# Graph attention in two layers: one fill order for the score banks, one exponential over two banks, and four smaller moves

## The chip, the cores and the metric

The kernel runs on one core of a Trainium2 chip. The metric is the time on the device in microseconds, as the median of several executions. Before the change it is 15735.61 us (three executions, 15734.61 to 15738.93).

## The reference: what is computed

Two layers on a graph of 3327 nodes with 128 features. The second one takes nearly all the time.

```python
# layer 0: attention by cosine, masked by the adjacency, residual, layernorm
cos = beta[0] * (x @ x.T) / (norm2 @ norm2.T + 1e-07)
x = _layernorm(x + softmax(cos + (1.0 - adj) * -1e9) @ x)
# layer 1: q, k, v have the shape (d, n, h) = (128, 3327, 8): 128 heads of 8 features
q = (x @ Wq.T).reshape(d, n, h)
k = (x @ Wk.T).reshape(d, n, h)
v = (x @ Wv.T).reshape(d, n, h)
a = einsum('dnh,dmh->dnm', q, k) * scale + adj + adj
out = einsum('dnm,dmh->dnh', softmax(a, axis=2), v)
x = _layernorm(x + out.reshape(n, h * d) @ Wo.T)
```

## The kernel before, in words

The nodes are padded to 26 tiles of 128. The work has four stages.

**Layer 0** (up to some 704 us) goes tile by tile through a pipeline written out by hand. Besides its own work it turns the adjacency (`adj_chunk`) and stores it in bf16 as `aT_s`, one DMA for each query tile, of 128 rows of 6,656 bytes (L215), and it stores q, k and v.

**Preparation** (704 to some 987 us): `prepare`, called 16 times, loads 16 heads of k or q (L796), lets GpSimd reorder them (L798), turns them on TensorE, splits each value into a high and a low part (L810, L811) and stores both (L818). Between its calls the adjacency of the first query block is loaded (L507) and exponentiated (L514), and the first maxima are searched for.

**The attention loop** (987 to some 15613 us) is the main stage. A unit is a block of query tiles with a group of four heads: 9 blocks by 32 groups make 288 units. Eight blocks have three tiles (384 query columns), the last has two (256). A unit has 26 steps, j = 0 to 25, one for each tile of 128 keys, so that there are 288 x 26 = 7488 steps. The maximum over the keys is needed before the scores can be exponentiated, so the scores are computed twice: once in a search for the maxima, which runs T + AHEAD = 33 steps ahead, and once to be used. The search for two units takes 52 steps, and each step searches one *pair* (two heads with 512 keys each, PSUM tile m2, two banks, L613) and one *single* (one head with 512 keys, PSUM tile m1, one bank, L634); `max_steps` lists which. In a two-tile block every second step has no pair. The maxima, negated and split into three bf16 parts by `shift_parts`, become the "shift" of a unit, which `shift_turn` turns on TensorE (L663) in the steps j = 22 to 24 of the unit before, into columns 384 to 511 of a bank of ea, out of which ScalarE copies it (L914, tile cx).

TensorE, ScalarE, VectorE and GpSimd execute exactly in the order in which the code issues (a manual schedule); only the DMA queue of SP is ordered by a scheduler. In a step TensorE's order is:

1. shifts of heads 2 and 3 into eb (two banks, L690), the first search, scores of heads 2 and 3 on top (L696). ScalarE exponentiates eb in one instruction (L893), and GpSimd multiplies by the exponentiated adjacency (L894).
2. shifts of heads 0 and 1 into ea (L690), the second search, scores on top (L696), perhaps L663 or L725, then twice the adjacency in eight matmuls, four for each head (L677). ScalarE exponentiates each of the two ea tiles with an instruction of its own (L923), then come the copies out of ea.
3. the weighing of the step before the last with the values (L707).

Heads 0 to 3 lie on four groups of 32 rows of the array, and the heads of a search on those of their own number. The first search is the pair if it is one of heads 0 and 1 (`early`), else the single. Of the 52 steps of a cycle, by the number s of the step modulo 52, the pair comes first in 6 to 31 and the single in the others. In steps 5 and 31 pair and single are on the same two heads. m1 and m2 have one buffer each; ea has two tiles of one bank, which are both in use in each step; eb has one tile of two banks.

When a unit is done, its sums are turned into the free columns of ea in the step j = 20 of the next unit (`values_turn`, L725) and finished in the same step: a copy on ScalarE (L737), a reciprocal on VectorE (L741), a product on GpSimd (L742), a store (L755). The keys of the unit after next are loaded at j = 2 (L530, L535, L542).

**The end** (15613 us on): for each of 26 tiles, eight transposes, copies, sixteen matmul instructions with Wo (L977) and the residual (L978). After the last tile come the rest of the layernorm over all tiles (`layernorm`, L133 to L141) and the store of the result (L983).

## Time and profile before

| | |
|---|---|
| median of three executions | 15735.61 us |
| the profiled execution | 15731.62 us |
| its span | 15729.8 us |
| share of the span busy: PE, DVE, ACT, POOL | 98%, 88%, 81%, 88% |
| layer 0, up to 704 us: DMA share | 0.43 |
| L893, 128x768 (6656 times): mean | 811 ns |
| L923, 128x384 (13312 times): mean | 490 ns |
| L613, 128x1024: mean | 1219 ns |
| L634, 128x512: mean | 684 ns |
| L894, 128x768: mean | 1843 ns |

PE is TensorE's matmuls, PEld its weight loads, DVE VectorE, ACT ScalarE, POOL GpSimd, SP the queue that issues the DMAs. A line such as "L893 ACT ACTIVATE pb<-eb" names the line of the code, the engine, the operation, what it writes and what it reads. Rows of the timeline begin with the start in us from the span's start and the duration in us; neighbouring instructions of one kind are merged ("x2"), and a bracket tells of the engine's idle time before it. Matmuls are pipelined, so that several of them overlap and the ends that the trace shows for them are modelled.

### The profile page before, as it was taken

Reading aid. Unit: us, or ns where it says so; the run is one execution under the profiler, and the core shown is the slowest. Engines: PE = TensorE matmul, PEld = TensorE weight load, DVE = VectorE, ACT = ScalarE, POOL = GpSimd, SP = SyncE. Lnnn points to the kernel's source line nnn. Section 1 sums busy time; section 2 is a strip of 40 time slices with the busy share of each in tenths; the row PEclk is TensorE's granted clock in tenths of the full one; section 3 lists DMA queues with packets and bytes.
Section 4 is the critical chain, followed back from the end, with each engine's and each line's share of the span. In section 5 each row is a group of like instructions: output and inputs, shape, how many; then the busy total and the mean of one; then the engine's idle time right before and its main releaser. Section 6 shows DMA issues by size and latency. Waiting matters only on the chain.

```text
span 15729.8 us, 508048 instructions
## 1 busy us (share of the span) xinstructions
PE 15442.3 (98%) x217532; PEld 6909.7 (44%) x217532; DVE 13882.2 (88%) x16261; ACT 12687.4 (81%) x24930; POOL 13894.1 (88%) x9571
## 2 busy tenths in 40 slices
PE   8879999999999999999999999999999999999999
PEld 6644444444444444444444444444444444444555
DVE  7679999999999999999999999999999999998775
ACT  7658888888888888888888888888888888888776
POOL 0059999999999999999999999999999999999886
PEclk9989999999999999999999999999999999999999
DMA  4451111111111111111111111111111111111112
GB/s 169 180 201 49 45 49 52 49 46 49 52 50 49 47 50 52 49 45 49 52 49 46 49 53 48 50 45 56 45 49 45 49 52 49 46 49 60 61 56 74
DMA packets 600521, 951.50 MB, mean 60 GB/s; under 512 B 283090, under 2 KB 515408, under 8 KB 557808
## 3 DMA queue, kind: packets, MB, share of 16 engines
q1 hardware_dynamic: 598256, 918.99, 18.0%
q8 instruction: 1703, 27.90, 0.7%
q14 instruction: 562, 4.60, 0.1%
HBM read 784.19 MB, written 134.61 MB: 58 GB/s over the span
## 4 chain that ended last, share of the span: by engine, by line
PE 91%; DVE 2%; ACT 1%; issue 0%; POOL 0%; DMA 0%; SPq 0%; ACTq 0%; DVEq 0%; POOLq 0%
PE acc L707 29%; PE ea L677 20%; PE m L598 15%; PE eb L690 12%; PE ea L690 9%; PE ea L696 2%; PE eb L696 2%; PE ea L663 1%; DVE mx L613 1%; PE ea L725 1%; DVE mx L634 1%; ACT pa L923 0%; PE pp L977 0%; POOL pb L894 0%; ACT pb L893 0%
## 5 line engine op out<-in xcount | busy, mean ns | idle before, releaser
L894 POOL TENSOR_TENSOR pb<-pb,eT 128x768 f32<-128x768 f32 (+1 forms) x7488 | 13206.6, 1781 | 752.7 <-ACT pb L893 557.7
L613 DVE TENSOR_REDUCE mx<-m 128x2 f32<-128x1024 f32 x6784 | 8271.6, 1219 | 506.9 <-PE eb L696 283.1
L893 ACT ACTIVATE pb<-eb 128x768 f32<-128x768 f32 (+1 forms) x7488 | 5895.6, 787 | 2509.9 <-PE eb L696 1716.6
L598 PE MATMUL m<-kx,qx 32*128 32x512 f32 (+1 forms) x23296 | 6774.5, 471 | 85.9 <-DVE mx L613 78.2
L923 ACT ACTIVATE pa<-ea 128x384 f32<-128x384 f32 (+1 forms) x14976 | 6339.0, 478 | 56.5 <-PE ea L677 43.5
L707 PE MATMUL acc<-pb,vt 128*9 128x384 f32 (+1 forms) x29952 | 5904.2, 474 | 0.1
L707 PE MATMUL acc<-pa,vt 128*9 128x384 f32 (+1 forms) x29952 | 5903.3, 474 | 0.0
L634 DVE TENSOR_REDUCE mx<-m 128x1 f32<-128x512 f32 x6400 | 4377.6, 684 | 682.2 <-PE m L598 316.3
L690 PEld LDWEIGHTS <-one 3*128 3x128 bf16 x29952 | 1508.1, 91 | 5553.9 <-issue 4650.8
L677 PE MATMUL ea<-aT,two 128*32 128x384 bf16 (+1 forms) x59904 | 3716.2, 325 | 0.0
L696 PE MATMUL eb<-qx,kx 32*128 32x384 f32 (+1 forms) x14976 | 3444.5, 452 | 0.0
L696 PE MATMUL ea<-qx,kx 32*128 32x384 f32 (+1 forms) x14976 | 3439.1, 437 | 0.0
L690 PE MATMUL ea<-cx,one 3*128 3x384 bf16 (+1 forms) x14976 | 3293.0, 322 | 2.3
L598 PEld LDWEIGHTS m<-kx,qx 32*128 32x128 f32 x23296 | 2813.9, 182 | 443.7 <-DVE mx L613 123.0
L690 PE MATMUL eb<-cx,one 3*128 3x384 bf16 (+1 forms) x14976 | 2462.7, 326 | 1.3 <-ACT pb L893 0.6
L707 PEld LDWEIGHTS acc<-pa,vt 128*9 128x9 f32 x29952 | 1416.7, 91 | 781.5 <-issue 0.3
L677 PEld LDWEIGHTS <-two 128*32 128x32 bf16 x59904 | 947.0, 95 | 1415.6 <-issue 1273.6
L696 PEld LDWEIGHTS eb<-qx,kx 32*128 32x128 f32 x14976 | 1461.7, 189 | 0.0
L696 PEld LDWEIGHTS ea<-qx,kx 32*128 32x128 f32 x14976 | 1433.1, 182 | 8.0 <-issue 3.0
L707 PEld LDWEIGHTS acc<-pb,vt 128*9 128x9 f32 x29952 | 1418.8, 91 | 0.6 <-POOL pb L894 0.6
L638 DVE TENSOR_REDUCE mx<-m 128x2 f32<-128x512 f32 x1088 | 747.9, 687 | 96.3 <-PE eb L696 38.2
L116 POOL MEMSET raw<- 128x1 f32 x26 | 2.4, 98 | 559.0 <-DVE mn L260 478.2
(126 smaller groups left out, 5253.8 us busy)
## 6 DMA issues: line engine op xcount, KB each, us to landing
kx<-kp_s SPq DMA_DIRECT2D x576, 832.0 KB
vn<-v_s SPq DMA_DIRECT2D x288, 416.0 KB
qx<-qp_s SPq DMA_DIRECT2D x1024, 48.0 KB
raw<-in_adj_dram SPq DMA_DIRECT2D x25, 1663.5 KB
aT_s<-aT SPq DMA_DIRECT2D x26, 832.0 KB
aT<-aT_s SPq DMA_DIRECT2D x208, 96.0 KB
q_s<-row SPq DMA_DIRECT2D x26, 512.0 KB
k_s<-row SPq DMA_DIRECT2D x26, 512.0 KB
```

Of the source, the lines that this page charges most:

```text
L598: nc.tensor.matmul(dst, u.qx[rows(a), q * P : (q + 1) * P], u.kx[rows(a), k0:k1], start=True, stop=True,)
L613: nc.vector.tensor_reduce(u.mx[:, h, qs[0], c], m, axis=AX.X, op=ALU.max)
L634: nc.vector.tensor_reduce(u.mx[:, a, qs[0], c : c + 1], m, axis=AX.X, op=ALU.max)
L638: nc.vector.tensor_reduce(u.mx[:, a, qs[0] : qs[1] + 1, c], m.rearrange("p (q k) -> p q k", q=2), axis=AX.X, op=ALU.max,)
L663: nc.tensor.matmul(dst[r], parts[u.i % 2][:, q, h], unit, start=start, stop=True, tile_position=(0, 32 * h), skip_group_check=True,)
L677: nc.tensor.matmul(e[r, : u.nq], two[:, r], aT[:, j, : u.nq], start=False, stop=True, tile_position=(0, 32 * c), skip_group_check=True,)
L690: nc.tensor.matmul(e[:, : u.nq], one[r], u.cx[r, : u.nq], start=True, stop=False, skip_group_check=True)
L696: nc.tensor.matmul(e[:, : u.nq], u.kx[rows(a), j * P : (j + 1) * P], u.qx[rows(a), : u.nq], start=False, stop=stop, skip_group_check=True,)
L707: nc.tensor.matmul(acc[32 * h : 32 * h + H + 1, : u.nq], u.vt[:, h, j], pts[h // 2][:, h % 2, : u.nq], start=(j == 0), stop=(j == T - 1), ...
L893: nc.scalar.activation(pt_b[:, :, : u.nq], e_b[:, :, : u.nq], AF.Exp)
L894: nc.gpsimd.tensor_tensor(pt_b[:, :, : u.nq], pt_b[:, :, : u.nq], eT[:, j, : u.nq].unsqueeze(1).to_broadcast([P, 2, u.nq]), ALU.mult,)
L923: nc.scalar.activation(pt_a[:, h, : u.nq], e[:, : u.nq], AF.Exp)
```

## The change

It has five parts.

1. **Fill order.** In three-tile blocks the pair is always the first search, and the single the second. The pair's heads are now those of ea (`hs_a`), and the other two those of eb (`hs_b`), so that ea and eb change heads when the pairs do. The list of singles is reordered so that no single has a head of the pair beside it. In the two-tile block the order stays as it was: single first, pair second, eb with heads 2 and 3.
2. **One exponential.** ea becomes one tile of two banks with one buffer, and one ACTIVATE exponentiates both.
3. **The sums of a finished unit** are turned at j = 8 in place of 20, with their copy (`leave`), and the reciprocal and what follows (`finish`) come one step later, at j = 9.
4. **Loads.** `aT_s` is laid out by query block, so that a store of one query tile is made of pieces of 256 bytes, and a load of one key tile of pieces of 768 bytes in place of 256. In the preparation the heads are loaded two calls ahead, and the loads of the adjacency are spread over four calls, seven tiles in each.
5. **The end.** The layernorm is done tile by tile inside the loop, and the first 20 tiles are stored while the last six are computed.

```diff
-    aT_s = dram.tile([T, P, T, P], BF16, name="aT_s")
+    aT_s = dram.tile([NB, P, T, QT * P], BF16, name="aT_s")
...
     def layernorm(dst: bass.AP, src: bass.AP):
-        stats = small.tile([P, T, nc.vector.BN_STATS_DIM], F32, name="ln_stats", bufs=1)
...
+        stats = small.tile([P, nc.vector.BN_STATS_DIM], F32, name="ln_stats")
+        mv = small.tile([P, nc.vector.BN_AGGR_DIM], F32, name="ln_mv")
+        rstd = small.tile([P, 1], F32, name="ln_rstd")
+        nc.vector.bn_stats(stats, src)
+        nc.vector.bn_aggr(mv, stats)
+        nc.vector.tensor_scalar(rstd, mv[:, 1:2], EPS, None, op0=ALU.add)
         nc.scalar.activation(rstd, rstd, AF.Sqrt)
         nc.vector.reciprocal(rstd, rstd)
...
             if c == NCH - 1:
-                nc.sync.dma_start(aT_s[t], u.aT)
+                q = t % QT
+                nc.sync.dma_start(aT_s[t // QT][:, :, q * P : (q + 1) * P], u.aT)
...
-            nc.sync.dma_start(
-                aT[:, j, :w].rearrange("p (q n) -> p q n", n=P),
-                aT_s[b * QT : b * QT + w // P, :, j].rearrange("q p n -> p q n"),
-            )
+            nc.sync.dma_start(aT[:, j, :w], aT_s[b][:, j, :w])
...
             pairs = [(u, lo, *k) for k in full[:12]] + [(u, lo, (2,), 6)]
-            ones = one(u, hi, full[13:] + [left]) + one(u, lo, full[12:] + [left])
+            last = one(w, hi, full[12:] + [left])
+            ones = one(u, hi, full[13:] + [left]) + last[:1] + one(u, lo, full[12:] + [left])
             pairs += [(u, hi, *k) for k in full[:13]] + [(u, hi, (2,), 6)]
             pairs += [(w, hi, *k) for k in full[:12]]
-            ones += one(w, lo, full[13:] + [left])
             pairs += [(w, lo, *k) for k in full[:13]]
-            ones += one(w, hi, full[12:] + [left])
+            ones += one(w, lo, full[13:] + [left]) + last[1:]
...
+        def search(step):
+            if step is not None:
+                (max_pair if len(step[1]) == 2 else max_single)(*step)
...
-                    pts[h // 2][:, h % 2, : u.nq],
+                    pts[h][:, : u.nq],
...
+        def leave(u, src):
+            u.of = sm.tile([P, QT, 4, H + 1], F32, name="of")
+            nc.scalar.copy(u.of[:, : u.nt].rearrange("p q h r -> p (q h r)"), src[:, : 36 * u.nt])
+
+        def finish(u):
+            by = u.of.rearrange("p q h r -> p h q r")[:, :, : u.nt]
...
+                load_heads(0)
+                load_heads(1)
+                for i in range(len(works)):
+                    prepare(i)
...
+                    if i % 2 and i < 9:
+                        for j in range(7 * (i // 2), min(7 * (i // 2) + 7, T)):
                             load_adj_tile(0, j)
...
-            ps_a = at.enter_context(tc.tile_pool(name="at_a", bufs=2, space=PSUM))
+            ps_a = at.enter_context(tc.tile_pool(name="at_a", bufs=1, space=PSUM))
...
             def new_a():
-                return [ps_a.tile([P, 512], F32, name="ea") for _ in range(2)]
+                return ps_a.tile([P, 2, 512], F32, name="ea")
...
-                    early = pair is not None and pair[1] == (0, 1)
+
+                    full = pair is not None and width(units[pair[0]][0]) == QB
+                    first = pair if full else single
+                    late = single if full else pair
+                    hs_a = pair[1] if full else (0, 1)
+                    hs_b = tuple(h for h in range(4) if h not in hs_a)
...
-                    shifts(u, b01, (2, 3))
-                    if early:
-                        max_pair(*pair)
-                    elif single is not None:
-                        max_single(*single)
-                    scores(u, j, b01, (2, 3), True)
+                    shifts(u, b01, hs_b)
+                    search(first)
+                    scores(u, j, b01, hs_b, True)
...
-                    e_a = new_a()
-                    shifts(u, e_a, (0, 1))
-                    if early:
-                        max_single(*single)
-                    elif pair is not None:
-                        max_pair(*pair)
-                    scores(u, j, e_a, (0, 1), False)
+                    both = new_a()
+                    e_a = [both[:, x] for x in range(2)]
+                    shifts(u, e_a, hs_a)
+                    search(late)
+                    scores(u, j, e_a, hs_a, False)
...
-                    if j == T - 6 and done is not None:
+                    if j == 8 and done is not None:
                         values_turn(done, free, False)
-                        copies.append(lambda: finish(done, free))
+                        copies.append(lambda: leave(done, free))
+                    if j == 9 and done is not None:
+                        copies.append(lambda: finish(done))
...
-                    for h, e in enumerate(e_a):
-                        nc.scalar.activation(pt_a[:, h, : u.nq], e[:, : u.nq], AF.Exp)
+                    nc.scalar.activation(pt_a[:, :, : u.nq], both[:, :, : u.nq], AF.Exp)
...
-            nc.vector.tensor_add(hid[:, t, :], pp, x1)
-        res = big.tile([P, T, D], F32, name="res")
-        layernorm(res, hid)
-        rf = res.rearrange("p t d -> p (t d)")
+            hid = work.tile([P, D], F32, name="hid1")
+            nc.vector.tensor_add(hid, pp, x1)
+            layernorm(res[:, t, :], hid)
+            if t == HALF - 1:
+                nc.sync.dma_start(node_blocks(out, slice(0, P), HALF * D), rf[:, : HALF * D])
```

## The prediction

> **What bounds the kernel now.** I read the totals of the page, then busy time by stage, then the timeline of single steps in two places.
>
> ```profile
> span 15729.8 us, 508048 instructions
> PE 15442.3 (98%) x217532; PEld 6909.7 (44%) x217532; DVE 13882.2 (88%) x16261; ACT 12687.4 (81%) x24930; POOL 13894.1 (88%) x9571
> ```
>
> PE is near its span, but its matmuls overlap, so 98% doesn't say that PE is the limit. By stage (columns: length, busy PE, PEld, DVE, ACT, POOL, clock, DMA share, GB/s):
>
> ```profile
> 704.00:987.00 283.00, 127.79 (x554) 92.46 (x554) 135.93 (x215) 76.50 (x145) 51.37 (x30) 0.62 0.95 332
> 987.00:14260.00 13273.00, 13250.56 (x189309) 5562.42 (x189309) 12121.84 (x13742) 10969.24 (x21304) 12629.08 (x8394) 1.00 0.16 49
> 14260.00:15613.00 1353.00, 1352.35 (x23517) 686.47 (x23509) 1027.61 (x1327) 1090.90 (x2770) 1195.59 (x1101) 1.00 0.18 56
> ```
>
> The time lies in the second row: 256 units of three query tiles, 6656 steps of 2.00 us on average. The third row is the last 32 units, of two tiles. The first is the preparation, bound by DMA (share 0.95). What limits a step is seen in a steady pair of them:
>
> ```profile
> 8001.88 0.34 PE L690 MATMUL eb<-cx,one 3*128 3x384 bf16 x2
> 8001.89 0.50 PE L598 MATMUL m<-kx,qx 32*128 32x512 f32 x2
> 8002.43 1.23 DVE L613 TENSOR_REDUCE mx<-m 128x2 f32<-128x1024 f32 x1
> 8003.58 0.68 DVE L634 TENSOR_REDUCE mx<-m 128x1 f32<-128x512 f32 x1
> 8004.31 0.49 PE L598 MATMUL m<-kx,qx 32*128 32x512 f32 x1
> 8005.82 0.34 PE L690 MATMUL eb<-cx,one 3*128 3x384 bf16 x2
> ```
>
> It is a ring: pair matmuls to pair reduction 0.54, to single reduction 1.15, to the single matmul that waits for bank m1 0.73, to the start of the next-but-one step 1.51. That is 3.94 us for two steps, 1.97 each. Neither DVE nor PE is full; the ring through both sets the pace.
>
> In the steps j = 22 to 24 ScalarE also copies the next unit's shifts (L914) out of the bank that the score tile ea lies in, and another ring is in force:
>
> ```profile
> 7290.25 0.50 PE L598 MATMUL m<-kx,qx 32*128 32x512 f32 x1
> 7290.74 0.50 PE L677 MATMUL ea<-aT,two 128*32 128x384 bf16 x8
> 7291.19 0.87 ACT L923 ACTIVATE pa<-ea 128x384 f32<-128x384 f32 x2
> 7291.95 0.27 ACT L914 CAST cx<-ea 128x128 bf16<-128x128 f32 x1
> 7292.17 0.42 PE L690 MATMUL ea<-cx,one 3*128 3x384 bf16 x2
> 7292.27 0.50 PE L598 MATMUL m<-kx,qx 32*128 32x512 f32 x1
> ```
>
> From single to single 0.94 + 0.76 + 0.32 = 2.02 us: the first exponential starts 0.45 us after the adjacency matmuls begin, and the second shift of the next step waits until the copy has left the bank.
>
> **What the skill says.** "ScalarE: Activation LUTs", section on what ACT_TABLE_LOAD costs: an ACTIVATE without pointer operands takes 186 ns and 0.833 ns per element, and neighbours overlap by some 93 ns. The trace agrees: 0.811 us for 768 elements (826 by the page), 0.49 for 384, overlap 0.11. So one exponential over two banks saves only 2 x 0.49 - 0.11 - 0.81 = 0.06 us of ScalarE. "TensorE: Matmul & The Clock Gate", Part 3 (the mechanism): matmuls on different row groups run together. The trace agrees: L598 starts 7 ns behind L690. "DMA: Bandwidth & Descriptors", Specifications: below 512 B a transfer falls short of line rate. The trace has 18 ns for packets of 256 B against 254 ns for 6,656 B, 1.8 times the time per byte.
>
> **The change, part by part** (against the profiled execution, 15731.6 us; its span lacks 1.8 us of that, and the median of the three runs, 15735.6, lies 4.0 above it).
>
> *Constant fill order and singles off the pair's heads.* The ring has the same length in either order: steps s mod 52 = 6 to 17 (pair first) average 1.970 us from one L893 start to the next, 32 to 45 (single first) 1.965. Only the crossings cost. Over the 128 cycles of 52 steps (two units, counted from the first one's step 0), steps 4 and 5 take 4.45 where two take 3.94, steps 30 to 33 take 8.37 where four take 7.87: 1.01 us. Step 30 has four short matmuls that remain, 0.1; and the half with pair first is 0.27 us longer than the other without its crossing, and will now come twice. I take 0.80 gone per cycle (bounds 0.65 and 0.92): 128 x 0.80 = **-102**.
>
> *One exponential over two banks.* It waits for both heads' adjacency matmuls. These start in two groups of four, 0.17 us apart (row by row in the trace), so where PE ends the wait it starts 0.17 later, and both banks come free together. Queued behind it on ScalarE are the copies and the next L893; for the banks PE waits with the next ea shifts, and behind those stand the single, the scores, the adjacency and the weighing, that is, the whole step. In the copy ring: 0.94 + 0.17 = 1.11 to the exponential, 0.81 - 0.11 = 0.70 to the copy, 0.32 + 0.02 to the next single: 2.15 against 2.02. Three such intervals a unit: 256 x 3 x 0.13 = **+100**. In plain steps this ring is 0.63 (ea shift to the last add) + 0.44 + 0.81 + 0.05 (end of the exponential to the shift it frees) = 1.93, under the 1.97 of the other: nothing, but with 0.04 us to spare. That cover is thin: each 0.01 beyond it costs up to 6656 x 0.01 = 67.
>
> In the two-tile units the ring already shows: in a step without a pair the second ea shift starts 0.05 us after the second exponential ends.
>
> ```profile
> 14751.04 0.66 ACT L923 ACTIVATE pa<-ea 128x256 f32<-128x256 f32 x2
> 14751.40 0.28 PE L690 MATMUL eb<-cx,one 3*128 3x256 bf16 x2
> 14751.47 0.55 PE L690 MATMUL ea<-cx,one 3*128 3x256 bf16 x2
> ```
>
> One exponential of 512 elements starts 0.12 later (14751.16), takes 0.60 as L893's does there, and frees both at 14751.81 where the second shift started at 14751.75. With 0.01 in the other step: 0.07 per two steps, 416 x 0.07 = +30; the copies of two steps in 32 units, 64 x 0.13 = +8: **+38**.
>
> *Values turned at j = 8, finished at 9.* L725 costs the same PE time, 0.22, at either place. Its copy holds the bank, so step 9 gets the 0.13 of the copy ring, which step 21 had in part: +0.15 us. The reciprocal L741 no longer waits for ScalarE (58 us in 162 waits in the three-tile units); behind it on DVE the pair reduction was late by 0.07. Net +0.09 for each of 256 units: **+23** (bounds -20 and +45).
>
> *Layout of aT_s, loads two ahead.* Each store of a tile in the first layer becomes 3328 pieces of 256 B instead of 128 of 6,656: 3328 x 18 / 16 = 3.7 us of all engines against 2.0. Today it lands 3.4 us after its issue and the next write into its buffer comes some 16.8 us after that issue: hidden, with 13 us to go; it also sits ahead of nothing urgent, as the raw tiles land 20 us early. On SP nothing is reordered in the main loop but o_s<-ob, now ahead of vn, which waits longer anyway. In the preparation the first adjacency loads fall from 9984 packets of 18 ns to 3328 (768 B, an estimate of 37 from 39 at 832 B): -3.5; the earlier loads fill gaps of a stage that is 0.95 full, at most 15. A load two ahead waits on SP for GpSimd to have emptied its buffer, with the stores of the piece in hand behind it; those need the output of the same copy, so they lose nothing. I take **-5** (bounds -15 and +5).
>
> *Layernorm tile by tile.* The chain ends in 26 L141 in a row, 6.5 us, then 1.66 MB out in 6.9. Afterwards one L141 and six tiles' bytes are left: -6.2 and about -4 (0.39 MB at 330 GB/s instead of 1.66), +1.3 where the table load, hidden today, comes in front of a copy. DVE has room: 1.3 us of new work in a period of 3.355. **-9**.
>
> Sum: -102 + 100 + 38 + 23 - 5 - 9 = +45: **15780**.
>
> **Rivals.** *The crossings win* (chance 0.18). If the joint exponential starts no later than the pair of them (ScalarE busy until then, as in steady steps where L893's end holds it back), the +100, the +30 and the +8 vanish and the reciprocal's gain stays: 15735.6 - 102 - 20 - 14 = 15600. For it: in the shorter step of a plain pair the first exponential starts at the end of L893 (8005.30 after 8004.60 + 0.81, less the overlap). Against it: in the copy steps and the two-tile units it starts 0.45 and 0.40 after the adds begin.
> *The ea ring becomes the bound everywhere* (0.12). It decides from 1.97 per step, that is if the joint exponential starts over 0.04 later than I put it: at 0.06 more it is 1.99, and some 40 of 52 steps lose 0.02: 128 x 40 x 0.02 = +102, so 15882. Speaking for it: shift, score, add, exponential are one buffer deep.
> *The crossings stay* (0.08): where the heads change sides the first step could stall just as now; 15780 + 102 = 15882.
>
> **How the numbers follow.** The forecast holds with 0.62, between 15690 and 15850: sums of the bounds above (-16 and +20 for the crossings, +-40 for the copies, +-45 for the finish, partly cancelling). About 0.2% (31 us) is what a measurement of this kernel can tell from no change. Slower by more than that: 0.38 of the forecast's 0.62, and the two slow rivals: 0.58. Within: 0.20. Faster: the rival's 0.18 and 0.04 of the forecast: 0.22. Signs are mixed, so the range reaches out: 15620 to 15880.
>
> **What would show it.** Right: steps 4, 5 and 31 at the length of the others; copy steps of 2.15 us, the two-tile pair of steps 3.10 instead of 3.03; joint exponentials of 0.81 whose start stands 0.44 after the last add; the last L141 some 1.5 us after the last matmul. Wrong: copy steps still at 2.02 (then the first rival), plain steps above 1.97 with PE's ea shifts waiting for the exponential (the second), DVE waits as many as now (the third), or time gained or lost ahead of 987 us by more than 15.

## The result and the profile after

The changed kernel takes **15764.5 us** (median of 20 runs, 15757.6 to 15773.0) against 15734.6 for the kernel before (20 runs, 15731.3 to 15739.9): ratio **1.0019**, 95% interval 1.0012 to 1.0026. It is 30 us slower where 45 were forecast (15780). The profiled execution took 15766.6 us.

The totals of the page are nearly those of before; only the number of instructions fell, by one exponential a step.

```profile
span 15764.8 us, 500738 instructions
PE 15460.4 (98%) x217532; PEld 7036.6 (45%) x217532; DVE 13904.7 (88%) x16311; ACT 12722.1 (81%) x17467; POOL 13895.4 (88%) x9571
```

So the reading has to be by stage again. I cut the stages at the first exponential of eb (L905, L893 before), at the first of the two-tile units and at the last. Columns: length, busy PE, PEld, DVE, ACT, POOL, clock, DMA share, GB/s.

```profile
704.00:996.27 292.27, 141.86 (x569) 97.48 (x569) 137.48 (x216) 77.64 (x148) 51.38 (x30) 0.58 0.94 322
996.27:14351.13 13354.86, 13303.24 (x190378) 5721.43 (x190374) 12183.94 (x13808) 11076.19 (x14792) 12702.69 (x8447) 1.00 0.16 49
14351.13:15659.25 1308.12, 1303.45 (x22436) 651.27 (x22432) 976.50 (x1261) 1013.82 (x1794) 1123.33 (x1048) 1.00 0.18 54
```

Before, the same cuts give 988.4 to the first exponential, 13346.6, 1278.0 and a tail of 116.9. So the 35 us between the two profiled spans are +7.8 ahead of the loop, +8.3 in the three-tile units, +30.2 in the two-tile units, and -11.3 in the tail (105.6).

The small +8.3 is a sum of large terms. The crossings, the steps at which pair and single used to change places, no longer cost time: the starts of L905 in steps 4, 5 and 6 of one cycle stand 1.92 and 2.02 us apart. In the same cycle of the kernel before they stood 2.17 and 2.28 apart, with ScalarE idle for up to 0.70 ahead of them. Before, then after:

```profile
7254.15 0.81 ACT L893 ACTIVATE pb<-eb 128x768 f32<-128x768 f32 x1 [0.40 <-PE m L598]
7256.32 0.81 ACT L893 ACTIVATE pb<-eb 128x768 f32<-128x768 f32 x1 [0.59 <-PE m L598]
7258.60 0.81 ACT L893 ACTIVATE pb<-eb 128x768 f32<-128x768 f32 x1 [0.70 <-PE m L598]
```

```profile
7265.52 0.81 ACT L905 ACTIVATE pb<-eb 128x768 f32<-128x768 f32 x1 [0.30 <-PE eb L692]
7267.44 0.81 ACT L905 ACTIVATE pb<-eb 128x768 f32<-128x768 f32 x1 [0.29 <-PE eb L692]
7269.46 0.81 ACT L905 ACTIVATE pb<-eb 128x768 f32<-128x768 f32 x1 [0.30 <-PE eb L692]
```

A copy step (one in which ScalarE copies a shift of the next unit out of ea), in the timeline of the same kernel:

```profile
7301.13 0.50 PE L590 MATMUL m<-kx,qx 32*128 32x512 f32 x1
7301.62 0.50 PE L673 MATMUL ea<-aT,two 128*32 128x384 bf16 x8
7302.23 0.81 ACT L934 ACTIVATE pa<-ea 128x768 f32<-128x768 f32 x1
7302.94 0.26 ACT L924 CAST cx<-ea 128x128 bf16<-128x128 f32 x1
7303.25 0.34 PE L686 MATMUL ea<-cx,one 3*128 3x384 bf16 x2
7303.26 0.50 PE L590 MATMUL m<-kx,qx 32*128 32x512 f32 x1
```

From single to single 2.13 us: 0.49 to the adds, 0.61 to the joint exponential, 0.71 to the copy, 0.32 to the next single. The joint exponential starts when the second group of adds is through, the copy stands behind it, and TensorE's next shift into ea stands behind the copy. Before, the same interval was 2.02.

Two-tile steps, same view:

```profile
14669.78 0.60 ACT L905 ACTIVATE pb<-eb 128x512 f32<-128x512 f32 x1 [0.29 <-PE m L590]
14669.88 0.40 PE L673 MATMUL ea<-aT,two 128*32 128x256 bf16 x8
14670.40 0.60 ACT L934 ACTIVATE pa<-ea 128x512 f32<-128x512 f32 x1
14671.05 0.28 PE L686 MATMUL ea<-cx,one 3*128 3x256 bf16 x1
...
14671.39 0.60 ACT L905 ACTIVATE pb<-eb 128x512 f32<-128x512 f32 x1 [0.40 <-PE m L590]
...
14672.88 0.60 ACT L905 ACTIVATE pb<-eb 128x512 f32<-128x512 f32 x1 [0.29 <-PE m L590]
```

The pair of steps takes 3.10 us, and the next shift into ea comes 0.05 after the joint exponential's end (14671.00).

### The profile page after: what moved, and what is told of

It reads as the page before. It is cut to its first block, busy times and chain, and to the rows that moved or that the text cites. A ratio compares the mean times of both kernels' runs of the same rounds, so it can differ in the third digit from the quotient of the medians.

```text
span 15764.8 us, 500738 instructions
## 1 busy us (share of the span) xinstructions
PE 15460.4 (98%) x217532; PEld 7036.6 (45%) x217532; DVE 13904.7 (88%) x16311; ACT 12722.1 (81%) x17467; POOL 13895.4 (88%) x9571
## 4 chain that ended last, share of the span: by engine, by line
PE 92%; ACT 1%; issue 0%; DVE 0%; DMA 0%; POOL 0%; ACTq 0%; SPq 0%; POOLq 0%; DVEq 0%
PE acc L703 29%; PE ea L673 20%; PE m L590 15%; PE eb L686 12%; PE ea L686 12%; PE ea L692 2%; PE ea L659 1%; PE eb L692 1%; ACT pa L934 1%; PE ea L721 1%; ACT pb L905 0%; PE pp L994 0%; DVE oT L147 0%; DMA qp_s<-low 0%; PE tp L157 0%
## 5 line engine op out<-in xcount | busy, mean ns | idle before, releaser
L905 ACT ACTIVATE pb<-eb 128x768 f32<-128x768 f32 (+1 forms) x7488 | 5894.0, 787 | 1975.5 <-PE eb L692 1218.8
L590 PE MATMUL m<-kx,qx 32*128 32x512 f32 (+1 forms) x23296 | 6944.4, 473 | 80.4 <-DVE mx L605 72.1
L934 ACT ACTIVATE pa<-ea 128x768 f32<-128x768 f32 (+1 forms) x7488 | 5896.6, 787 | 599.6 <-PE ea L673 283.1
L686 PEld LDWEIGHTS <-one 3*128 3x128 bf16 x29952 | 1825.0, 91 | 5841.7 <-issue 4753.9
L686 PE MATMUL ea<-cx,one 3*128 3x384 bf16 (+1 forms) x14976 | 2487.7, 319 | 55.4 <-ACT pa L934 9.2
## 6 DMA issues: line engine op xcount, KB each, us to landing
raw<-in_adj_dram SPq DMA_DIRECT2D x25, 1663.5 KB, 6.5
```

The lines of the kernel that those rows point to most:

```text
L590: nc.tensor.matmul(dst, u.qx[rows(a), q * P : (q + 1) * P], u.kx[rows(a), k0:k1], start=True, stop=True,)
L686: nc.tensor.matmul(e[:, : u.nq], one[r], u.cx[r, : u.nq], start=True, stop=False, skip_group_check=True)
L905: nc.scalar.activation(pt_b[:, :, : u.nq], e_b[:, :, : u.nq], AF.Exp)
L934: nc.scalar.activation(pt_a[:, :, : u.nq], both[:, :, : u.nq], AF.Exp)
```

## The experiments

All times are medians; ratios are to the kernel before, run on the same chip (15730.4 to 15732.0 there, up to 4 us under the 15734.6 that the changed kernel was compared with). Two tables carry the verdicts. The first is read like the windows above, from the starts of the exponential of eb; its last column is the median of all executions, the others are of the profiled one. The second is read from the mean distances of these starts at each of the 52 places of a cycle (two units), summed over the places named. A cycle occurs 128 times.

```
kernel                  first exp  three-tile  two-tile  tail    total
before                    988.4     13346.6     1278.0   116.9   15734.6
after                     996.3     13354.9     1308.1   105.6   15764.5
e8_order_alone            983.5     13236.6     1277.5   117.3   15615.6
e2_joint_alone            983.7     13453.5     1306.5   116.5   15866.7
e5_values_moved           987.5     13334.3     1279.3   117.1   15721.3
e6_outside_loop           998.6     13344.3     1278.3   106.0   15720.7
e1_two_exps               992.4     13231.2     1280.2   105.9   15617.3
e7_two_exps_old_prep      991.5     13235.9     1279.9   105.8   15618.1
e4_old_order              987.8     13456.4     1308.1   105.8   15865.5
e3_copy_elsewhere         996.6     13248.1     1298.4   105.4   15647.9
e9_joint_held             991.1     13336.7     1300.9   105.4   15735.1
e10_two_exps_held         997.6     13251.6     1294.3   105.2   15648.3
e11_joint_in_plain        988.4     13416.0     1358.4   106.5   15876.6
e12_two_exps_one_wait     987.9     13218.3     1271.5   105.1   15587.0
```

```
us per cycle        steps 4,5,30-33  22-25,48-51  8,9,34,35  20,21,46,47  other 30
                    (crossings)      (copies)     (values)
before                  12.82          16.19        7.87        8.33        59.06
after                   11.85          16.78        8.50        8.08        59.13
e8_order_alone          11.82          16.17        7.88        8.43        59.11
e2_joint_alone          12.79          16.81        7.87        8.56        59.08
e5_values_moved         12.82          16.14        8.09        8.05        59.07
e1_two_exps             11.82          16.14        8.30        8.03        59.07
e4_old_order            12.79          16.77        8.41        8.06        59.10
e3_copy_elsewhere       11.85          15.93        8.53        8.07        59.11
e9_joint_held           11.83          16.77        8.49        8.03        59.08
e10_two_exps_held       11.82          16.25        8.30        8.05        59.10
e11_joint_in_plain      11.85          17.12        8.63        8.11        59.10
e12_two_exps_one_wait   11.85          16.00        8.18        8.11        59.12
```

The last column is the first thing to see: 30 plain steps take 59.1 us, 1.97 each, in every kernel. No edit here moved them by more than 0.07 us in 59. That the ring through the search is their limit, as the prediction has it, is read from the timelines: no edit here changes that ring.

### The exponential split again in the changed kernel (e1_two_exps)

```
-            ps_a = ...(name="at_a", bufs=1, space=PSUM)
+            ps_a = ...(name="at_a", bufs=2, space=PSUM)
...
-                return ps_a.tile([P, 2, 512], F32, name="ea")
+                return [ps_a.tile([P, 512], F32, name="ea") for _ in range(2)]
...
-                    nc.scalar.activation(pt_a[:, :, : u.nq], both[:, :, : u.nq], AF.Exp)
+                    for h, e in enumerate(e_a):
+                        nc.scalar.activation(pt_a[:, h, : u.nq], e[:, : u.nq], AF.Exp)
```

> The changed kernel with one edit undone: two exponentials of one bank each, as before, in place of the joint one; the fill order, the choice of heads, the moved values, the preparation and the tail stay as changed. My theory (the order gains, the joint exponential gives it back): by the terms on record 15764.5 - 100 - 38 = 15627 us; sized by the two traces instead (copy steps' excess 1.02 us per cycle of 52 steps against 0.43, two-tile units +30): 15764.5 - 128 x 0.59 - 30 = 15659. Copy steps 2.02 to 2.06, two-tile pair of steps 3.03. Rival (the joint exponential costs nothing, and the order gains less than its crossings show): 15765, all steps as in the changed kernel.

Measured: 15617.3 us (15611.7 to 15623.0), ratio 0.9928 (0.9915 to 0.9940). A copy step, from its timeline:

```profile
7239.31 0.50 PE L673 MATMUL ea<-aT,two 128*32 128x384 bf16 x8
7239.76 0.87 ACT L934 ACTIVATE pa<-ea 128x384 f32<-128x384 f32 x2
7240.52 0.27 ACT L923 CAST cx<-ea 128x128 bf16<-128x128 f32 x1
7240.73 0.42 PE L686 MATMUL ea<-cx,one 3*128 3x384 bf16 x2
```

From the adds to the first exponential 0.45 where the joint one needs 0.61, to the copy 0.76 where it needs 0.71. So the joint exponential, with the tile of two banks that it reads, costs 147 us of the changed kernel (144 if each is set against the kernel before on its own chip). The two profiled executions lie 155 apart: 124 in the three-tile units, 28 in the two-tile units, and 4 ahead of the loop, where this edit does nothing. The order's gain was there all along.

### The joint exponential alone (e2_joint_alone)

The same edit, the other way round, in the kernel before (with one buffer in place of two):

```
-                return [ps_a.tile([P, 512], F32, name="ea") for _ in range(2)]
+                return ps_a.tile([P, 2, 512], F32, name="ea")
...
-                    for h, e in enumerate(e_a):
-                        nc.scalar.activation(pt_a[:, h, : u.nq], e[:, : u.nq], AF.Exp)
+                    nc.scalar.activation(pt_a[:, :, : u.nq], both[:, :, : u.nq], AF.Exp)
```

> The kernel before with one edit alone: the score tile ea as one tile of two banks and one exponential over it. My theory: 15734.6 + 100 + 38 = 15873 us by the terms on record, 15734.6 + 76 + 30 = 15841 as sized by the traces; the crossings stay at 4.45 and 8.37 us or grow a little. Rival (the joint exponential costs nothing): 15735. A second rival (in the half with the single first, where the second search of a step is the pair, the joint exponential's later end stalls plain steps too): above 15900.

Measured: 15866.7 us, ratio 1.0087 (1.0073 to 1.0100), +136. The copy steps grow by 0.62 per cycle, the two-tile units by 28.5 us, the plain steps not at all: the second rival is out.

### The old order in the changed kernel (e4_old_order)

```
-            last = one(w, hi, full[12:] + [left])
-            ones = one(u, hi, full[13:] + [left]) + last[:1] + one(u, lo, full[12:] + [left])
+            ones = one(u, hi, full[13:] + [left]) + one(u, lo, full[12:] + [left])
...
-                    hs_a = pair[1] if full else (0, 1)
-                    hs_b = tuple(h for h in range(4) if h not in hs_a)
+                    early = pair is not None and pair[1] == (0, 1)
+                    first, late = (pair, single) if early else (single, pair)
+                    hs_a, hs_b = (0, 1), (2, 3)
```

> The changed kernel with one edit undone: the fill order of before (pair first in half of the steps, single first in the other, heads 0 and 1 always in ea); the joint exponential and all else stay. My theory: the crossings come back, + 102: 15867 us; steps 4, 5 at 4.45 together and 30 to 33 at 8.37. Rival (crossings were paid for elsewhere, in the half with the pair first, and the order is worth nothing): 15765.

Measured: 15865.5 us, ratio 1.0086 (1.0072 to 1.0099). The crossing is back, here at steps 4 and 5, 2.14 and 2.28 us. The brackets show ScalarE idle for up to 0.77 ahead of the exponential of eb, where it was 0.30 in the changed kernel, and the search's matmul (L589) as what it came behind:

```profile
7305.07 0.81 ACT L902 ACTIVATE pb<-eb 128x768 f32<-128x768 f32 x1 [0.30 <-PE eb L691]
7307.21 0.81 ACT L902 ACTIVATE pb<-eb 128x768 f32<-128x768 f32 x1 [0.51 <-PE m L589]
7309.49 0.81 ACT L902 ACTIVATE pb<-eb 128x768 f32<-128x768 f32 x1 [0.77 <-PE m L589]
```

The order is worth 101.6 us (13456.44 - 13354.86) in the three-tile units, with joint exponential and moved values.

### The order alone (e8_order_alone)

The edit of e4 the other way round in the kernel before; two exponentials and values at j = 20 stay:

```
-            ones = one(u, hi, full[13:] + [left]) + one(u, lo, full[12:] + [left])
+            last = one(w, hi, full[12:] + [left])
+            ones = one(u, hi, full[13:] + [left]) + last[:1] + one(u, lo, full[12:] + [left])
...
+                    hs_a = pair[1] if full else (0, 1)
+                    hs_b = tuple(h for h in range(4) if h not in hs_a)
```

> The kernel before with one edit alone: the constant fill order with heads assigned so that singles keep off the pair's heads; two exponentials, values at j = 20, preparation and tail as before. My theory: -102: 15633 us, steps 4, 5 and 30 to 33 at 1.97 on average. Rival (the gain of the order depends on the values having left j = 20, where steps 46, 47 with the reversed heads already take 4.09 without them): 128 x 0.15 = 20 less of it, 15653.

Measured: 15615.6 us, ratio 0.9928 (0.9914 to 0.9942), -115; 110 us of it in the three-tile units. The rival has its 0.10 in steps 20, 21, 46, 47 (8.43), but the crossings give 1.00. Alone the order gains 0.86 per cycle; once the values have moved, steps 8, 9, 34 and 35 take 8.30 with it and 8.09 without, and its gain is 1.00 - 0.21 + 0.02 = 0.81. The edit has three things in it: which search comes first, which heads lie in ea, and the order of the singles. No run takes them apart, so which of them removes the stall is not shown.

### The copies read from elsewhere (e3_copy_elsewhere)

```
-                            lambda: nc.scalar.copy(x.cx[:, q * P : (q + 1) * P], free)
+                            lambda: nc.scalar.copy(x.cx[:, q * P : (q + 1) * P], ident)
```

> The changed kernel, but the copies of the next unit's shifts read the identity tile in SBUF (128 x 128) and not the score bank; the matmuls that turn the shifts into the bank stay. So the shifts of every unit but the first are not the ones that the reference asks for. My theory (the copy holds the bank of the joint exponential, and the next shifts of ea wait for it): copy steps fall from 2.14 to 1.97 to 2.00, 256 x 3 x 0.15 = 115 less: 15650 us. Rival (it is ScalarE's own time for the copy, or the turning matmuls on TensorE, that lengthen these steps): within 20 us of 15765.

Measured: 15647.9 us, ratio 0.9947 (0.9934 to 0.9961), 117 less than the changed kernel. ScalarE still copies 128 x 128 behind the joint exponential, TensorE still turns the shifts into the bank, but the next shift starts when the exponential ends (7251.50 + 0.81 = 7252.31) and not when the copy does (7252.50):

```profile
7251.50 0.81 ACT L934 ACTIVATE pa<-ea 128x768 f32<-128x768 f32 x1
7252.21 0.29 ACT L924 CAST cx<-ident 128x128 bf16<-128x128 f32 x1
7252.36 0.34 PE L686 MATMUL ea<-cx,one 3*128 3x384 bf16 x2
```

So it is the hold on the bank and not ScalarE's time. These 117 us are the price of the whole hold, more than the joint exponential adds to it: with two exponentials the copy steps take 16.14 us per cycle, with the joint one 16.78, and with the joint one but without the hold 15.93.

### The values moved alone (e5_values_moved)

```
-                    if j == T - 6 and done is not None:
+                    if j == 8 and done is not None:
                         values_turn(done, free, False)
-                        copies.append(lambda: finish(done, free))
+                        copies.append(lambda: leave(done, free))
+                    if j == 9 and done is not None:
+                        copies.append(lambda: finish(done))
```

> The kernel before with one edit alone: the values turned at j = 8 and finished at j = 9, where they were turned and finished at j = 20. By the terms on record: 15734.6 + 23 = 15758 us. Sized by the runs so far (with two exponentials and the new order, steps 8, 9 take 4.11 together and 34, 35 take 4.19; before, steps 20, 21 take 4.23 and 46, 47 take 4.10): 128 x (8.30 - 8.33), that is nothing: 15735. Rival (the reciprocal no longer holds up the pair reduction, and nothing else changes): 15734.6 - 20 = 15715.

Measured: 15721.3 us, ratio 0.9995 (0.9987 to 1.0003): not to be told from no change by its total; by stage -12.3 in the three-tile units. Steps 8, 9, 34, 35 take 0.22 more, and steps 20, 21, 46, 47 give back 0.28; the copy steps give another 0.05.

### What lies outside the loop (e6_outside_loop, e7_two_exps_old_prep)

The first has the new layout of aT_s, the loads two ahead and the layernorm by tiles in the kernel before; the second is e1_two_exps with the old layout and loads:

```
-    aT_s = dram.tile([NB, P, T, QT * P], BF16, name="aT_s")
+    aT_s = dram.tile([T, P, T, P], BF16, name="aT_s")
...
-                load_heads(0)
-                load_heads(1)
-                for i in range(len(works)):
-                    prepare(i)
+                for g in range(NG):
+                    for src, dst in ((k_s, kp_s), (q_s, qp_s)):
+                        prepare(g, src, dst)
```

> The kernel before with the edits outside the loop alone: the layout of aT_s, the loads two ahead, the layernorm tile by tile. By the terms on record: 15734.6 - 5 - 9 = 15721 us. Sized by the runs so far (first GpSimd copy of the preparation to first exponential: 258.2 us in the two runs with the old preparation, 260.3 to 263.8 in the four with the new; tail 105.4 to 105.9 against 116.5 to 116.9): 15734.6 + 3.4 - 11 = 15727. Rival (the preparation is bound by its transfers and costs nothing more; the +3.4 is chance): 15723.

> The best version if the preparation lost: the changed kernel with two exponentials again, and with the layout of aT_s and the loads of before; order, moved values and tail stay as changed. If the new preparation costs 3.4 us: 15617 - 3 = 15614 us. By the term on record (the new one gains 5): 15622. A difference under 5 us is within what these runs can tell.

Measured: 15720.7 us, ratio 0.9994 (0.9986 to 1.0002), and 15618.1 us, 0.9 from e1_two_exps. The tail is 11 us shorter in every kernel that has the new layernorm. The gain in the preparation isn't there: the totals show none, and the first exponential stands at 993.0 us in the mean of nine profiles with the new preparation (987.8 to 998.6) and at 986.9 in the five with the old one (983.5 to 991.5). Of these 6 us, 3.8 lie between the last layernorm of the first layer and the end of its projections, where the granted clock falls to about a half at a moment that differs from run to run. In the changed kernel it falls within the first projection of K, at 696.6 us: a pair of matmuls of L346 takes 1.12 us from 694.56, 1.88 from 696.37 and 2.07 from 698.94.

In five of the fourteen profiles it doesn't fall before the projections end, two with the new preparation among them. The Trainium skill ("TensorE: Matmul & The Clock Gate", section What's actually happening) says that the clock is set by an activity window that runs freely, not tied to the kernel's start, so that the moment of a transition varies, by half a microsecond in the page's measurement. Here the first fall lies anywhere from 696 to 717 us, so the profiles agree that it varies, but that window alone isn't shown to explain so wide a spread. Whether the new loads make it fall earlier stays open.

### Holding ea a little longer (e9_joint_held, e10_two_exps_held)

A probe of how much room the plain steps have, in the changed kernel and, with the same line behind the two exponentials, in e1_two_exps.

```
                     nc.scalar.activation(pt_a[:, :, : u.nq], both[:, :, : u.nq], AF.Exp)
+                    nc.scalar.copy(held, e_a[1][:, :1])
```

> The changed kernel with a probe added: in every step, right behind the joint exponential, ScalarE copies one column of ea (128 x 1, about 0.19 us, of which some 0.11 overlaps its neighbour), so the banks come free about 0.08 us later. My theory (in plain steps the ring through ea is 1.93 us, 0.04 under the search ring's 1.97): it passes to 2.01, so 44 plain steps of 52 lose 0.04, the 8 steps with copies or values 0.08, the two-tile steps about 0.07: 128 x (1.76 + 0.64) + 832 x 0.07 = 365 more: 16130 us. Rival (plain steps have more room than that, at least 0.08): 128 x 0.64 + 58 = 140 more: 15905. Rival (they have none): 6656 x 0.08 + 58 = 590 more: 16355.

> The same probe in the kernel with two exponentials (e1_two_exps). There the second exponential ends 0.17 + 0.81 - 0.49 - 0.38 = 0.11 us earlier, so the ring is 1.82 and with the probe 1.90: plain steps lose nothing, the 8 steps with copies or values up to 0.08 each, two-tile steps up to 0.05: at most 82 + 42 more than 15617, so 15617 to 15741, most likely 15720 us. Rival (what counts is ScalarE's own time and not the ring, or the ring is as long as with the joint exponential): as much more as in the joint case, some 365: 15980.

Measured: 15735.1 us (ratio 1.0004, 0.9996 to 1.0013) and 15648.3 us (0.9947, 0.9932 to 0.9962). The second lies in its range, 31 more than e1_two_exps (20 in the three-tile units, 14 in the two-tile ones). The first is **29 us faster than the changed kernel** (25 if each is set against the kernel before on its own chip), against all three theories. Its timeline says why:

```profile
7269.64 0.16 ACT L937 COPY held<-ea 128x1 f32<-128x1 f32 x1
7269.84 0.34 PE L686 MATMUL ea<-cx,one 3*128 3x384 bf16 x2
7269.97 0.50 PE L590 MATMUL m<-kx,qx 32*128 32x512 f32 x1
...
7270.39 0.51 PE L673 MATMUL ea<-aT,two 128*32 128x384 bf16 x8
7270.95 0.81 ACT L936 ACTIVATE pa<-ea 128x768 f32<-128x768 f32 x1
```

The probe does hold the bank: the shift comes 0.05 after its end. But the joint exponential starts 0.56 after the first add where it started 0.61 after it. Over the plain steps of the loop the median from the last add's start is 0.377 here and 0.438 in the changed kernel, with hardly any spread (0.003 between the 5th and the 95th percentile). The answer of the trace on the exponential's line, first in the changed kernel, then with the probe, names the difference:

```profile
L934 ACT ACTIVATE pa<-ea x7488: 591/811/825, 997.0 to 15660.0; 128x768 f32<-128x768 f32 x176, 128x512 f32<-128x512 f32 x22
L934 ACTq EVENT_SEMAPHORE  x7484: 17/17/17, 1006.8 to 15659.9; - x197
  PE ea L673: 283.1, 1320
```

```profile
L936 ACT ACTIVATE pa<-ea x7488: 591/811/836, 991.8 to 15629.3; 128x768 f32<-128x768 f32 x176, 128x512 f32<-128x512 f32 x22
  PE ea L673: 112.0, 613
```

In the changed kernel (and before, for the first of two exponentials) the exponential waits for two things: TensorE, and ScalarE's own earlier work, presumably for the reuse of pa's buffer. In the trace an extra instruction on ScalarE's queue takes the wait for TensorE, the exponential keeps the other, and it starts 0.062 us behind the extra one. The probe waits for ScalarE's own work itself; the exponential then waits for TensorE alone, and the extra instruction is gone. The exponential of eb keeps its own (7489 in each of these kernels), so the difference doesn't come from there. The Trainium skill ("Perfetto Trace Analysis", section Identifying Dependency Chains) has the mechanism: an instruction that waits on several engines may have such instructions put ahead of it. Here it is worth 0.06 us per exponential. So the probe took 0.06 off the ring and put 0.05 on it, and said nothing of the room in plain steps. In e10_two_exps_held the extra instruction of L936 is gone as well, so its 31 us are the price of the hold less that gain.

### Two exponentials in a two-bank tile (e11_joint_in_plain)

```
-                    nc.scalar.activation(pt_a[:, :, : u.nq], both[:, :, : u.nq], AF.Exp)
+                    if copies or u.nq < QB:
+                        for h, e in enumerate(e_a):
+                            nc.scalar.activation(pt_a[:, h, : u.nq], e[:, : u.nq], AF.Exp)
+                    else:
+                        nc.scalar.activation(pt_a[:, :, : u.nq], both[:, :, : u.nq], AF.Exp)
```

> The changed kernel, but the joint exponential only in steps of the three-tile units that have no copy behind it; two exponentials where shifts or values are copied, where the reciprocal is issued, and in the two-tile units. The tile stays one of two banks, so both are released together. My theory (plain steps lose nothing by the joint exponential): all but some 20 us of what e1_two_exps gained comes back: 15640 us. Rival (the joint exponential costs its time in plain steps, 6656 x 0.01 to 0.02): above 15690.

Measured: 15876.6 us, ratio 1.0092 (1.0077 to 1.0107), 112 **more** than the changed kernel (116 on each one's own chip): my expectation failed, and not through plain steps (59.10 as ever).

```profile
7322.94 0.50 PE L673 MATMUL ea<-aT,two 128*32 128x384 bf16 x8
7323.55 0.87 ACT L936 ACTIVATE pa<-ea 128x384 f32<-128x384 f32 x2
7324.31 0.27 ACT L924 CAST cx<-ea 128x128 bf16<-128x128 f32 x1
7324.63 0.34 PE L686 MATMUL ea<-cx,one 3*128 3x384 bf16 x2
```

The first of the two starts 0.61 after the first add, as the joint one does, not 0.45: with both banks in one tile its wait is for the last add of both. Then two exponentials take 0.87 where one takes 0.81, and each copy step is 0.06 longer (2.20): 61 us in the three-tile units and, with such a pair in every step, 50 in the two-tile ones. So what costs time is that two banks are **one tile**, filled before either is read and freed together; given that tile, one exponential is the better choice.

### The version that the runs point to (e12_two_exps_one_wait)

Against e1_two_exps:

```
                     for f in copies:
                         f()
+                    nc.scalar.copy(held, ident[:, :1])
```

> The kernel with two exponentials (e1_two_exps), and at the end of every step's ScalarE work a copy of one column of the identity tile into a scratch tile. It holds no bank; by its being there the first exponential of the next step no longer has a second wait, on ScalarE's own semaphore, and starts 0.38 instead of 0.44 us after the last add of its bank, as seen in e9_joint_held. My theory: the 8 steps of 52 whose exponentials wait for the adds (copies, values) gain 0.05 each, 128 x 8 x 0.05 = 51, two-tile steps about 0.03 each, 832 x 0.03 = 25, plain steps nothing: 15617 - 76 = 15541 us. Rival (the extra instruction's 0.08 us on ScalarE delays the next exponential of eb as much as the wait cost, or another wait of the step ends last there): 15617 or a little more.

Measured: **15587.0 us** (15584.6 to 15593.4), ratio 0.9908 (0.9892 to 0.9925): 145 us under the kernel before, 178 under the changed one, 30 under e1_two_exps. Of these 30, the profiled executions show 22 in the loop and 4.5 ahead of it, where the edit does nothing; 76 were expected.

```profile
7228.06 0.50 PE L673 MATMUL ea<-aT,two 128*32 128x384 bf16 x8
7228.45 0.87 ACT L936 ACTIVATE pa<-ea 128x384 f32<-128x384 f32 x2
7229.21 0.27 ACT L925 CAST cx<-ea 128x128 bf16<-128x128 f32 x1
7229.49 0.36 PE L686 MATMUL ea<-cx,one 3*128 3x384 bf16 x2
```

In this copy step the first exponential starts 0.39 after the adds (0.45 in e1_two_exps), and of the 7484 extra instructions ahead of it none is left. Copy and value steps gain 0.14 and 0.12 per cycle, 33 us together; but steps 20, 21, 46, 47, the crossings and the others give back 0.08, 0.03 and 0.05, 20 us. The two-tile units gain 9 us, not 25. The mechanism is shown. The size was too large for two reasons: steps that I had taken to be unaffected lose, and not every copy step gains its start. At the places 23 and 50 of the cycle the exponential starts 0.46 after the adds (0.45 in e1_two_exps), 0.707 behind the start of eb's exponential: there ScalarE's own work ends last, as the rival had it for these steps.

## Why the prediction was right, step by step

*Crossings, -102.* Measured -101.6 with the other parts in place (0.79 per cycle where I took 0.80), -110 alone. The forecast let 0.21 of the stall of 1.01 come back, for the short matmuls of step 30 and because the half with the pair first was longer (by 0.27, it says; the means of the places give 0.16, or 0.26 with the 0.1 of step 30 in it). What comes back, 0.15 to 0.22, is in other steps than I thought (46 and 47, or 8, 9, 34 and 35).

*Copy ring, +100.* Right in mechanism: the interval is 2.13 in the timeline where 2.15 was worked out, and it goes when the copy no longer holds the bank (e3). The joint exponential adds 0.64 per cycle in these steps, 82 us where 100 were forecast; with 26 in the steps with the values, which I had booked under those, and 16 in all others, the three-tile units' share is 124. The 107 us that e3 gains in these units are no measure of the term: they include what the copies cost with two exponentials already.

*Plain steps, nothing.* Confirmed: 59.06 to 59.13 us for 30 steps in fourteen kernels. The cover is as thin as the forecast put it, as a pair of plain steps of the changed kernel shows:

```profile
7280.42 0.81 ACT L934 ACTIVATE pa<-ea 128x768 f32<-128x768 f32 x1
7281.28 0.34 PE L686 MATMUL ea<-cx,one 3*128 3x384 bf16 x2
7281.30 0.50 PE L590 MATMUL m<-kx,qx 32*128 32x512 f32 x1
7282.35 0.81 ACT L934 ACTIVATE pa<-ea 128x768 f32<-128x768 f32 x1
7283.31 0.50 PE L590 MATMUL m<-kx,qx 32*128 32x512 f32 x1
7284.36 0.81 ACT L934 ACTIVATE pa<-ea 128x768 f32<-128x768 f32 x1
```

The steps alternate, 1.93 and 2.01 us. In every plain step of the three-tile units the shift into ea starts 0.05 after the joint exponential's end, which the prediction had named with longer steps as the sign of its second rival; the steps aren't longer, because the single behind the shift has to wait for its bank as well, and follows it by up to 0.03 in the short steps and 0.07 to 0.10 in the long ones (medians by place). The short step is the ring through ea at its length of 1.93. Two of them would be 3.85 where a pair takes 3.94, so 0.045 a step is left. What happens when that is used up was not tried: the probe, which was to do it, shortened the ring by 0.01.

*Two-tile units, +38.* Measured +28 to +30. Set place by place against e1, the pairs of steps without a copy are 0.064 longer (0.07 forecast), and those with one 0.086: so the copies add 1 to 2 us and not the 8 that were forecast. (The 9.7 us by which e3 is shorter here are again the whole hold of the copies on the bank, most of which e1 pays too.) The steady pairs go from 3.028 to 3.093.

*Values moved, +23.* The term furthest off. In the three-tile units it is -12 alone (e5), -1 and -5 with the order (e7 and e1 against e8), and +3 with the joint exponential (e4 against e2), which is the setting of the forecast. I charged the new place with the copy ring, rightly, and credited the old one with the reciprocal's wait and a part of the copy; but the old place gave back 0.28 to 0.50 per cycle, about what the new one took (0.22 to 0.54).

*Preparation, -5.* Not found; nothing to at most some us of loss, with the clock's moment mixed in. The first adjacency loads are the 3328 packets of 768 bytes that were forecast, but a packet took 46 ns in the mean (36 in the median, 37 estimated) against 18.5 for each of the 9984 before, so that they save 1.9 us of all engines and not 3.5. Why the stage shows nothing even of that stays open.

*Layernorm, -9.* Measured -11.3. After the last tile's matmuls with Wo only that tile's layernorm is left to do:

```profile
15757.03 2.05 PE L994 MATMUL pp<-wo,oT 128*128 128x128 f32 x16 [0.43 <-DVE oT L147]
...
15760.61 0.35 DVE L139 TENSOR_SCALAR res<-hid,ln_mv,ln_rstd 128x128 f32<-128x128 f32 x1
```

That is 1.9 us from the matmul's end, 1.5 forecast. (The 1.66 MB of the forecast are 1,663.5 KB of 1024 bytes, that is 1.70.)

The sum came within 15 us partly by luck: the errors of the terms lie on both sides, and the two largest cancel. The mechanisms of the two large terms, order and joint exponential, were right and were shown by taking each out and putting each in alone. Between the two profiled spans, taking the edits in the order e8, e1, after: order -110 (forecast -102), values -5 (+23), joint exponential +124 (+100), two-tile units +30 (+38), ahead of the loop +8 (-5), tail -11 (-9); together +35 with the roundings. The errors of the terms are about 10 us with their signs and 83 without. Of the rivals, the first (no cost of the joint exponential) fails on its start, 0.44 after the last add; the second on the plain steps; the third on steps 4 and 5.

## What to carry to other kernels

Joining instructions across buffers joins the buffers' life too: both fill before either is read and both come free at the end. Where the buffer is one deep, that lengthens the ring through it, and it costs time in the steps where this ring sets the pace (here some 140 us, nearly all of it outside the plain steps); the instruction saved, 0.06 us of an engine that isn't full, doesn't make up for it. A change of several parts that moves little can hide a gain and a loss of over 100 us each; undo the parts one at a time, and keep the part that pays. Check which steps a term touches at the place that is vacated as well as at the new one.

## What was not expected of the hardware

A second wait on an instruction cost 0.06 us of start here: the joint exponential starts 0.438 us after the last add's start with an extra semaphore instruction of 17 ns ahead of it, and 0.377 without it. So adding an instruction (0.15 to 0.22 us of ScalarE's time) to a queue that has room made the kernel faster, by 25 us in the loop with the joint exponential and by 22 with two (29 and 30 by the medians). It paid only in steps where nothing else held that exponential back: at the places 23 and 50 with two exponentials it started no earlier.
